# Ordering the second layer's first front, and the first transfers, inside the first layer's plan

## The chip, the core and the metric
The kernel runs on one core of one Trainium2 chip. The metric is the device time of one execution in microseconds, as the median of the runs. The engines named below are TensorE (PE, with its weight loads as PEld), VectorE (DVE), ScalarE (ACT), GpSimd (POOL) and SyncE (SP), which issues most of the DMAs; ACT issues the others. Each engine runs its instructions in the order in which the program gives them.

## What is computed
All data are float32: x is 32 batches of 128 tokens of 512. Layer 0 is a cross attention with 32 query heads and 8 key heads of width 16, layer 1 an RWKV block with a state per head of 16 x 16.
```python
# layer 0, per batch
q = x @ Wq + bq;  k = ctx @ Wk + bk;  v = ctx @ Wv + bv
attn = softmax(q k^T / sqrt(16) + mask)
x = layernorm((attn v) @ Wo + bo + x) * gamma + beta
# layer 1, time mixing
xn = ln1(x);  sx = shift(xn) - xn
xxx = xn + sx * maa_x
m = tanh(xxx @ maa_w1) by 5;  x_i = xn + sx * (maa_stack_i + m_i @ maa_w2_i)   # w, k, v, r, g
w = exp(-exp(time_decay + tanh(x_w @ decay_w1) @ decay_w2))
# per token: out = r (state + u k v);  state = w * state + k v
x = x + groupnorm(out) * silu(g) @ Wo
# layer 1, channel mixing
x = x + sigmoid(xr @ ffn_Wr) * (relu(xk @ ffn_Wk)^2 @ ffn_Wv)
```

## The kernel before
**Tiling.** The 32 batches go in 16 groups of two (NG, G), so most tiles are 128 partitions by 4 chunks by 256 tokens. Layer 0 (`attend`, L483) runs over all groups and leaves its rows in DRAM (`x1d`); layer 1 (`load1`, `front`, `recurrence`, `tail`, L977 to L1436) runs over all groups after it and loads these rows again.

**The planner.** Nothing is issued where it is written. `Plan.add` (L176) records a step: its engine, a cost in us, a function that issues its instructions, and the tiles that it reads and writes. `give_out` (L238) then simulates the five engines and issues the steps in the order which it finds; that order is kept on the chip, as it stands within `manual_schedule`. For each engine it takes, among the steps whose inputs are done and whose tiles have room, the one that can start without waiting 0.3 us or more, and among these the one with the lowest due. A due is the group's number plus an offset from a table written out by hand (WHEN0 at L34 for layer 0, WHEN1 at L68 for layer 1). A step of any engine but SP may be taken only if its due is no more than `ahead` (15.2739 in layer 0, 13.2672 in layer 1) over that of the oldest step still open. Layer 1's plan also lowers the dues of steps that others wait for, and gives places in the order of the dues (`turns`, L224); layer 0's plan does not.

**Two plans.** Layer 0's plan (`pl`) holds the attention alone and is given out whole; layer 1's plan is made after it, in tile pools taken after those of layer 0 are released. On each engine every step of the second plan therefore comes behind every step of the first.

**Around the junction.** The last steps of a group in layer 0 are: rd and bc (softmax sums to DRAM and back, SP L701, L707), oT (POOL L711), pw (PE L716), x (DVE L719), the norm (`norm`, L385: statistics on DVE, root on POOL), z (POOL L407, L721, L722) and the store of x1d (SP L724). A group of layer 1 begins with the load of its rows (x1t, SP L974) and state (s0), then `front` (L998): both norms, `shift` (L843: transposes pxnt, xnt on ACT, sxt on POOL), `mixed` (L888: xx on ACT and POOL), ph (PE L924), h (ACT L1009), the inputs x for i = 1 and 0 (`x5s`, L1010: px on PE L1025, DVE L1041, an add on POOL L1055), pdd (PE L1090) and hd (ACT L1095). The heavy projections follow: pk, pv, pr, pg (`project2`, PE L938), the inputs 2, 3 and 4, and the storing of v (vd, SP L1105), which the recurrence fetches again (kv, SP L1230).

**The start.** Outside the plan, SP loads ident, col, wk, wv, bk, ev, bv, the three rows, and prev; ACT loads wq and wo, and then the weights of layer 1 (w1, w2, wd1, wd2, wk1, wr1, wo1, wv1, wg1, fv). The loads of the plan (x, ct and m of each group) come behind those of SP. These instructions outside the plan are placed by the compiler between the plan's steps. wv1 and wg1 are loaded into `wtmp` (3 places, two chunks each) and copied by POOL (L759).

Of the kernel before, what the change touches and what calls it, by code (L numbers as in the profile page):

```python
# [8 lines left out]
F32 = mybir.dt.float32  # L9
# [5 lines left out]
P = 128  # L15
B = 32
# [19 lines left out]
        oT 0: -2.6252, oT 1: 3.3357, pT 0 0 0: -0.1744, pT 0 1 0: 1.2267, pT 1 0 0: -1.9192, pT 1 1 0: -0.8740,  # L36
        pr 0 0 0 0: 0.6529, pr 0 0 0 1: -0.0746, pr 0 0 1 0: -4.0682, pr 0 0 1 1: -0.1561, pr 0 1 0 0: 0.4501,
        pr 0 1 0 1: -0.3203, pr 0 1 1 0: -0.7878, pr 0 1 1 1: 0.0820, pr 1 0 0 0: 1.7871, pr 1 0 0 1: 2.2002,
        pr 1 0 1 0: -0.8730, pr 1 0 1 1: -1.8966, pr 1 1 0 0: -0.4270, pr 1 1 0 1: -2.0592, pr 1 1 1 0: 3.7724,
        pr 1 1 1 1: -0.8531, qT 0: -0.5042, qT 1: -0.0255, qT 2: -0.2635, qT 3: -1.0961, xT 0: 0.4768, xT 1: -0.1677  # L40
    """,
    "DVE": """
        kT 0: 1.2690, kT 1: -3.2473, mx 0 0 0: -1.1417, mx 0 0 1: -0.2864, mx 0 1 0: 1.2620, mx 0 1 1: -2.6166,
        mx 1 0 0: 2.6711, mx 1 0 1: -0.5335, mx 1 1 0: 1.7226, mx 1 1 1: -0.3724, pT 0 0 1: -1.2967, pT 0 0 2: 0.0513,
        pT 0 0 3: 0.0848, pT 0 1 1: -8.6724, pT 0 1 2: 0.0095, pT 0 1 3: -0.9150, pT 1 0 1: 0.2278, pT 1 0 2: 1.5335,
        pT 1 0 3: 0.1265, pT 1 1 1: -0.6521, pT 1 1 2: 0.0264, pT 1 1 3: -1.1512, pprev: -0.5247, pr 0 0 0: 3.0552,
        pr 0 0 1: -0.2034, pr 0 1 0: -6.8992, pr 0 1 1: 0.0841, pr 1 0 0: 3.8180, pr 1 0 1: 5.4106, pr 1 1 0: -0.1859,
        pr 1 1 1: -1.0387, pv: 1.4494, rT 0: 1.7614, rT 1: -6.4827, rs 0: 0.0025, rs 1: -1.3038, st a 0: 3.4819,
        st a 1: -0.7930, x 0: -1.6215, x 1: -0.7745
    """,  # L50
    "PE": """
        pk: -1.2090, po 0 0: -0.9547, po 0 1: -1.2559, po 1 0: 1.2553, po 1 1: -6.5573, ppT 0 0 0: -3.2574,
        ppT 0 0 1: -3.1897, ppT 0 0 2: 0.0759, ppT 0 0 3: -0.0050, ppT 0 1 0: -5.1850, ppT 0 1 1: -1.0390,
        ppT 0 1 2: -1.3378, ppT 0 1 3: -0.1908, ppT 1 0 0: -0.7659, ppT 1 0 1: 0.2863, ppT 1 0 2: -2.6538,
        ppT 1 0 3: -0.7327, ppT 1 1 0: -1.0396, ppT 1 1 1: -1.1030, ppT 1 1 2: -1.7141, ppT 1 1 3: -1.3304,
        pprev: 0.5587, pq 0: -0.5900, pq 2: -0.5203, pv: -0.7591, pw 0: -0.0622, pw 1: 0.0036, pxT 0: -1.1551,
        pxT 1: -1.2087, sc 0 0: -0.4025, sc 0 1: -0.1903, sc 1 0: 0.0128, sc 1 1: 0.3141
    """,
    "POOL": """
        oT 0: 1.2881, oT 1: 3.1556, sd a 0: -1.3405, sd a 1: -6.4837, x 0: -1.9469, x 1: 2.5134, z 0: -5.8626,  # L60
        z 1: -2.1882
    """,
    "SP": """
        bc 0: -0.4187, bc 1: -0.5237, ct 0: -1.3394, ct 1: -1.7142, m 0: -0.3457, m 1: 0.1999, rd 0: -8.2177,
        rd 1: 2.2127, x 0: -1.7606, x 1: -2.6917, z 0: 0.8576, z 1: -0.5330
# [4 lines left out]
        att 0: 8.9413, att 1: 10.3245, att 2: 10.9514, att 3: 4.2202, ew 0: 3.0530, ew 1: 7.1294, ew 2: 5.4799,  # L70
        ew 3: -0.1804, gt 0: 2.7896, gt 2: 7.2564, h0: 4.2793, hd: -0.7228, kk 0: 1.5652, kk 2: 8.9401,
        kv 0 0 0: 2.8237, kv 0 0 1: 2.8350, kv 0 1 0: 6.5988, kv 0 1 1: 4.7931, kv 1 0 0: 11.5248, kv 1 0 1: 12.1370,
        kv 1 1 0: 8.1713, kv 1 1 1: 8.4770, kv 2 0 0: 11.3074, kv 2 0 1: 0.7816, kv 2 1 0: 10.6862, kv 2 1 1: 7.1872,
        kv 3 0 0: 19.3264, kv 3 0 1: 5.1004, kv 3 1 0: 5.3317, kv 3 1 1: 6.5296, pk 0: 7.8527, pk 2: 3.7734,
        pv 0: 2.8655, pv 2: 13.4147, r 0: 10.0348, r 2: -0.1824, rr 0: 13.0999, rr 1: 2.8864, rstd: 5.6019,
        sq 0: -0.0986, sq 1: 8.8327, sq 2: 0.5974, sq 3: 5.6588, w4 0: 6.7771, w4 1: 3.1835, w4 2: 6.2518,
        w4 3: 1.3276, xnc 0: 5.1909, xnc 1: 3.5402, xnc 2: 5.5512, xnc 3: 9.4093, xnt 0: 4.3436, xnt 1: 6.3722,
        xnt 2: 7.1367, xnt 3: 8.6670, xx 0: 11.9355, xx 1: 6.5413, xx 2: 5.6875, xx 3: 9.8818, yk 0: 11.1356,
        yk 1: 1.7804, yk 2: 15.8112, yk 3: 13.9956, yr 0: 7.4657, yr 1: 8.8095, yr 2: 3.2938, yr 3: 8.7878,
        zc 0: 7.6581, zc 1: 0.9023, zt 0: 10.9657, zt 1: 5.2637  # L80
    """,
    "DVE": """
        a 0 0: -0.5883, a 0 1: -0.2414, a 0 2: 0.1043, a 0 3: 8.0118, a 1 0: 7.0047, a 1 1: 12.1762, a 1 2: 5.6912,
        a 1 3: 9.0685, a 2 0: 9.3322, a 2 1: 6.5083, a 2 2: 6.9110, a 2 3: 0.9712, a 3 0: 7.3177, a 3 1: 7.6874,
        a 3 2: 2.3097, a 3 3: 12.5406, ar 0 0: 2.4656, ar 0 1: 9.7666, ar 0 2: 5.7906, ar 0 3: 7.9178, ar 1 0: 6.6300,
        ar 1 1: 1.2202, ar 1 2: 6.5895, ar 1 3: 8.7855, ar 2 0: 28.3612, ar 2 1: 16.5392, ar 2 2: 12.3754,
        ar 2 3: 11.7973, ar 3 0: 9.1129, ar 3 1: 12.3189, ar 3 2: 9.0665, ar 3 3: 1.8400, gn 0: 8.4672, gn 1: 5.8193,
        gn 2: 3.6790, gn 3: 6.5194, gt 0: 0.0430, gt 2: -0.3529, own 0: 7.8602, own 1: 10.0300, own 2: 6.6987,
        own 3: 5.2960, pb 0: 0.7953, pb 1: 8.4093, pb 2: 4.1923, pb 3: 8.8563, raw 0: 2.2489, raw 1: 0.4033,
        raw 2: 5.9725, raw 3: 6.8204, rk 0: -0.4021, rk 1: 1.1444, rr 0: 7.1091, rr 1: 5.2378, rstd: 2.3485,  # L90
        st c 0: 6.9368, st c 1: 1.2521, st t 0: 8.7646, st t 1: 7.8543, x1c 0: 1.0294, x1c 1: 6.6954, x5 0 0: 2.9930,
        x5 0 1: 7.2539, x5 0 2: -1.0976, x5 0 3: 11.6924, x5 1 0: 8.4707, x5 1 1: -0.2943, x5 1 2: 10.2532,
        x5 1 3: 6.3221, x5 2 0: -0.6575, x5 2 1: 6.4713, x5 2 2: 12.8297, x5 2 3: 15.9903, x5 3 0: 6.5967,
        x5 3 1: 6.3600, x5 3 2: -0.8402, x5 3 3: -0.6696, x5 4 0: 8.4589, x5 4 1: 12.8956, x5 4 2: -0.4045,
        x5 4 3: 5.3981
    """,
    "PE": """
        acc 0: 13.3710, acc 1: 6.5427, acc 2: 6.5657, acc 3: 5.8187, pb 0: 18.0159, pb 2: 13.4697, pc 0: 0.6934,
        pc 1: 3.6234, pc 2: 5.2455, pc 3: 6.5762, pd 0: 1.0255, pd 1: 5.0703, pd 2: 6.9998, pd 3: 6.9286, pdd: 8.4674,
        pew 0: 6.2963, pew 2: 8.3876, pg 0: 1.2658, pg 2: 11.7555, ph0: 5.5651, pk 0: -0.5984, pk 2: -0.5853,  # L100
        pkk 0: 6.0318, pkk 2: 6.3700, pkv 0: 3.8400, pkv 1: 1.5996, pr 0: 0.4302, pr 2: -0.2452, prr 0: 3.2418,
        prr 1: 6.5661, pv 0: 20.6763, pv 2: -0.4713, pvar: 9.0706, pwo 0: 6.3422, pwo 1: 7.2520, px5 1 0: 6.5332,
# [226 lines left out]
def xattn_rwkv_kernel(  # L329
# [91 lines left out]
    with ExitStack() as sa:  # L421
# [8 lines left out]
        for tag in ("ln_st", "ln_mv", "ln_sd"):  # L430
            pl.tag(tag, 2)
# [1093 lines left out]
```

## Time and profile before
| | before |
|---|---|
| median of 3 runs | 2157.05 us (2153.24 to 2163.01) |
| the profiled execution | 2150.95 us, span 2149.2 us |
| busy: PE, PEld | 1992.6 us (93%), 1305.8 us (61%) |
| busy: DVE, ACT, POOL | 1783.0 us (83%), 1058.0 us (49%), 1294.0 us (60%) |
| mean granted clock of PE | 0.962 |
| DMA, mean rate | 252.23 MB, 117 GB/s |

The span runs from the first to the last instruction; some 2 us lie outside it. In the page's slices each digit is the busy share of one fortieth of the span (54 us) in tenths, and PEclk is the clock that the throttle granted to PE. A row of busy time by stretches gives, after the bounds and the length, for each engine the busy us and the number of instructions, then the granted clock, the mean busy share of the 16 DMA engines, and GB/s. A row of the timeline gives start, us, engine, line and operation, out<-in, and in brackets the idle time before it with what ended it; merged rows have one start and one length. "SPq" and "ACTq" are those engines' issuing of DMAs.

### The profile page before, as it was taken

The page shows a single profiled execution, that of the slowest core. Times are in us where ns is not written, and L with a number is a line of the kernel's source. Part 1 is how long each engine was busy: PE and PEld are TensorE (multiplying, and loading weights), DVE is VectorE, ACT ScalarE, POOL GpSimd, SP SyncE. Part 2 cuts the span into 40 slices and gives each one's busy share as a digit, 9 for nine tenths or more (in the row PEclk, how much of TensorE's full clock was granted, in tenths as well). Part 3 has the DMA queues.
Part 4 walks back from the last instruction along what each step waited for, and adds up shares of the span by engine and source line. Part 5 has one row for each costly group of instructions (what it writes and reads, how often), then busy time and mean ns, then how long its engine had stood idle before and what let it go on. Part 6 is the DMA issues. An engine that isn't in the chain of part 4 may idle for free.

```text
span 2149.2 us, 36169 instructions
## 1 busy us (share of the span) xinstructions
PE 1992.6 (93%) x11908; PEld 1305.8 (61%) x11908; DVE 1783.0 (83%) x2182; ACT 1058.0 (49%) x3473; POOL 1294.0 (60%) x1081
## 2 busy tenths in 40 slices
PE   5999999999958779999999999999999999999977
PEld 4666666666626546566675665656657566575643
DVE  3888888888844888989988899898988989888881
ACT  3888888888842233433434434344343443433332
POOL 1273334343345666777777777777777877777552
PEclk9999999999978889999999999999999999999988
DMA  7232221221024687887977978879788797886851
GB/s 207 61 127 66 62 70 60 68 61 60 27 81 80 114 121 114 146 158 122 175 122 138 167 117 168 130 138 163 120 161 134 141 165 117 162 136 115 163 99 59
DMA packets 155883, 252.23 MB, mean 117 GB/s; under 512 B 50512, under 2 KB 97648, under 8 KB 139312
## 3 DMA queue, kind: packets, MB, share of 16 engines
q1 hardware_dynamic: 149232, 240.27, 59.8%
q10 hardware_dynamic: 6464, 9.66, 1.4%
q8 instruction: 94, 1.54, 0.4%
q14 instruction: 93, 0.76, 0.1%
HBM read 224.12 MB, written 25.69 MB: 116 GB/s over the span
## 4 chain that ended last, share of the span: by engine, by line
PE 52%; DVE 7%; ACT 2%; DMA 1%; issue 1%; POOL 0%; SPq 0%; POOLq 0%; DVEq 0%; ACTq 0%
PE pkk L938 5%; PE pwo L956 5%; PE pk L938 5%; PE pv L938 5%; PE pr L938 4%; PE acc L1296 4%; PE pkv L956 4%; PE pg L938 4%; PE prr L956 4%; DVE a L1267 3%; PE pdd L1090 2%; PE px L1025 2%; DVE x L1041 2%; PE pc L1321 1%; PE pew L1162 1%
## 5 line engine op out<-in xcount | busy, mean ns | idle before, releaser
L1252 POOL TENSOR_TENSOR kv<-kv,kx 128x1016 f32<-128x1016 f32 x256 | 597.6, 2349 | 142.9 <-DMA kv<-vd 63.1
L1267 DVE TENSOR_TENSOR_SCAN a<-w,kv 128x1024 f32<-128x1024 f32 x256 | 587.3, 2294 | 29.1 <-ACT w L1191 8.0
L653 ACT ACTIVATE pr<-pr,mx 128x128 f32<-128x128 f32 x1024 | 398.3, 391 | 53.4 <-DVE mx L641 47.0
L1281 DVE TENSOR_TENSOR ar<-a,r 128x1024 f32<-128x1024 f32 x256 | 311.5, 1217 | 4.4
L1055 POOL TENSOR_TENSOR x<-x,xnt 128x512 f32<-128x512 f32 x160 | 187.2, 1181 | 92.1 <-DVE x L1041 79.4
L653 ACT ACTIVATION_READ_ACCUMULATOR pr<-pr,mx 128x1 f32 x1024 | 193.7, 189 | 0.0
L1041 DVE SCALAR_TENSOR_TENSOR x<-px,col,sxt 128x256 f32<-128x256 f32 x320 | 133.9, 473 | 59.5 <-PE pdd L1090 37.2
L629 DVE TENSOR_TENSOR pr<-sc,m 128x1024 f32<-128x1024 f32 x128 | 153.7, 1210 | 32.1 <-PE sc L613 29.0
L665 PE MATMUL ppT<-ident,pr 128*128 128x128 f32 x1024 | 154.3, 281 | 12.1 <-DVE pT L672 4.3
L665 PEld LDWEIGHTS ppT<-ident,pr 128*128 128x128 f32 x1024 | 115.4, 141 | 77.9 <-issue 25.9
L641 DVE TENSOR_REDUCE mx<-pr 128x8 f32<-128x1024 f32 x128 | 155.5, 1215 | 2.7
L1296 PE MATMUL acc<-ar,give 128*32 128x256 f32 x2048 | 142.5, 394 | 12.6 <-DVE ar L1281 12.6
L672 DVE COPY pT<-ppT 128x512 f32<-128x512 f32 x192 | 128.3, 682 | 22.9 <-PE ppT L665 18.2
L397 POOL TENSOR_SCALAR sd_a<-mv_a 128x1 f32<-128x1 f32 x32 | 7.1, 223 | 214.6 <-DVE mv_a L393 214.5
L716 PE MATMUL pw<-wo,oT 128*128 128x512 f32 x256 | 122.3, 610 | 9.8 <-POOL oT L711 8.8
L938 PE MATMUL pkk<-yk,fk 128*128 128x256 f32 x512 | 121.4, 392 | 6.2 <-POOL yk L905 6.2
L956 PE MATMUL pwo<-wo,gt 128*128 128x512 f32 x256 | 122.2, 612 | 5.0 <-ACT xnt L868 2.9
L938 PE MATMUL pr<-x,wr 128*128 128x256 f32 x512 | 122.0, 387 | 3.8 <-DVE x L1041 3.8
L557 PE MATMUL pq<-xT,wq 128*128 128x256 f32 x512 | 122.9, 389 | 0.7 <-ACT xT L512 0.7
L938 PE MATMUL pk<-x,wk 128*128 128x256 f32 x512 | 123.3, 390 | 0.0
L956 PE MATMUL pkv<-fv,kk 128*128 128x512 f32 x256 | 120.3, 603 | 0.0
L938 PE MATMUL pg<-x,wg 128*128 128x256 f32 x512 | 117.6, 383 | 2.9 <-DVE x L1041 2.9
(146 smaller groups left out, 3714.7 us busy)
## 6 DMA issues: line engine op xcount, KB each, us to landing
kv<-vd SPq DMA_DIRECT2D x1024, 128.0 KB
fk<-in_fWkT_dram SPq DMA_DIRECT2D x16, 1024.0 KB
fr<-in_fWrT_dram SPq DMA_DIRECT2D x16, 1024.0 KB
x<-in_x_dram SPq DMA_DIRECT2D x32, 256.0 KB
ct<-in_ctxT_dram SPq DMA_DIRECT2D x32, 256.0 KB
bc<-rd SPq DMA_DIRECT2D x256, 32.0 KB
x1d<-z SPq DMA_DIRECT2D x32, 256.0 KB
x1t<-x1d SPq DMA_DIRECT2D x32, 256.0 KB
```

Of the source, the lines that this page charges most:

```text
L629: lambda b=b, sc=sc, jp=jp, pr=pr: nc.vector.tensor_tensor(pr(), sc()[:, 2 * jp : 2 * jp + 2].rearrange("p j g e s -> p (j g e) s"), ms[b] ...
L641: lambda pr=pr, mx=mx: nc.vector.tensor_reduce(mx(), pr(), AX.X, ALU.max, negate=True),
L653: nc.scalar.activation(pr()[:, 4 * i + h, :], pr()[:, 4 * i + h, :], AF.Exp, bias=mx()[:, 4 * i + h : 4 * i + h + 1], accum_out=sm()[:, h0 ...
L665: nc.tensor.transpose(pt()[:, h, :], pr()[:, 4 * i + h, :], ident)
L938: nc.tensor.matmul(pp()[:, i], (w() if isinstance(w, Cell) else w)[:, kc, (c + i) * P : (c + i + 1) * P], flat(src()[:, kc]), start=(kc == 0),
L956: nc.tensor.matmul(pp(), src()[:, c, b, :], (w() if isinstance(w, Cell) else w)[:, c, :], start=(c == 0), stop=(c == KC - 1),)
L1041: lambda i=i, c=c, pp=pp, half=half: nc.vector.scalar_tensor_tensor(flat(ts[i]()[:, c]), pp()[:, half], col[:, MS0 + i, c : c + 1], flat(s ...
L1055: lambda i=i, c2=c2: nc.gpsimd.tensor_add(ts[i]()[:, c2 : c2 + 2].rearrange("p c b t -> p (c b) t"), ts[i]()[:, c2 : c2 + 2].rearrange("p ...
L1252: lambda c=c, kv=kv, e=e: nc.gpsimd.tensor_tensor(kv()[:, e, :, :, 1:T], kv()[:, e, :, :, 1:T], k()[:, c, :, 0 : T - 1].unsqueeze(1).broad ...
L1267: lambda kv=kv, a=a, e=e: nc.vector.tensor_tensor_scan(a().rearrange("p j b t -> p (j b t)"), w4().rearrange("p j b t -> p (j b t)"), kv() ...
L1281: lambda c=c, a=a, ar=ar: nc.vector.tensor_tensor(ar(), a().rearrange("p j b t -> p j (b t)"), flat(r()[:, c]).unsqueeze(1).broadcast_to([ ...
L1296: nc.tensor.matmul(acc()[32 * j : 32 * j + 32, :N], give[:, d].rearrange("p e h -> p (e h)"), tiles[d]()[:, j], start=(d == 0), stop=(d == 3),
```

## The change
Layer 1's plan object (`pl1`) and the pools of the tiles which the front needs are made before layer 0's, and layer 0's plan takes these pools in too: tags g, z, ln_st, ln_mv and ln_sd become shared, ct takes places of sx, and prev one of z. `front` becomes a generator that stops before the k projection. For group 0 its first part, with that group's loads, is added to layer 0's plan after all groups of the attention; the second part, inputs 2, 3 and 4 included, is added to layer 1's plan. The loads of wk, wv, wo, bk, ev, bv, rows and prev become steps of the plan on SP, and so do w1, w2, wd1 and wd2 (one step of six DMAs, moved from ACT's queue). Both tables of offsets and both `ahead` values are new; steps carry a default due, used where a table has no entry. `wtmp` has one place of one chunk.
```diff
@@ the tables (a few of the lines)
 WHEN0 = {
     "ACT": """
...
+        xT 0: -4.1567, xT 1: 1.6257, xnt 0: 17.9453, xnt 1: 13.6560, xnt 2: 9.3695, xnt 3: 16.3747, xx 0: 16.6506,
+        xx 1: 12.5462, xx 2: 9.3077, xx 3: 10.8186, zt 0: -0.6012, zt 1: 17.8612
...
+        pdd: 14.8434, ph0: 13.8237, pk: 1.1577, po 0 0: -4.9799, po 0 1: 2.0137, po 1 0: -2.0040, po 1 1: -4.7406,
...
+        ppT 0 1 1: 0.7530, ppT 0 1 2: -6.4545, ppT 0 1 3: -6.8061, ppT 1 0 0: -2.6161, ppT 1 0 1: -3.6615,
...
+        px5 1 0: 18.8360, px5 1 2: 17.3205, pxT 0: 0.9389, pxT 1: 1.0851, pxnt 0: 14.7081, pxnt 2: 16.4922,
...
+        bc 0: 3.2700, bc 1: -4.0132, bk: -1.2899, bv: 2.7605, ct 0: -0.5080, ct 1: -0.6118, m 0: 0.7228, m 1: 1.1452,
+        prev: 18.4768, rd 0: -1.5286, rd 1: -2.3089, rows: 0.9971, s0 0: 2.5007, s0 1: 17.0661, w1: 18.8761,
+        wk: -3.3755, wo: 11.9829, wv: 2.0257, x 0: -1.5799, x 1: -0.7466, x1t 0: 1.3447, x1t 1: -0.8892, z 0: -6.3176,
...
@@ Plan
-        s.due = s.group + self.when[s.key]
+        s.due = s.group + self.when.get(s.key, due - s.group)
...
     def give_out(self):
+        for _, _, live in self.pools.values():
+            live[:] = [c for c in live if any(u.end is None for _, _, u in c.uses)]
+            for c in live:
+                for _, _, u in c.uses:
+                    u.end = u.end and 3.4
@@ pools
+    pl1 = Plan(ctx, tc, WHEN1, 20.0126)
+    for tag, bufs in (("xt", 2), ("s0", 3), ("z", 3), ("xn", 2), ("sx", 2), ("x5", 4), ("h0", 1), ("hd", 1)):
+        pl1.tag(tag, bufs)
...
-        wt = sa.enter_context(tc.tile_pool(name="wt", bufs=3))
-        pl = Plan(sa, tc, WHEN0, 15.2739)
+        wt = sa.enter_context(tc.tile_pool(name="wt", bufs=1))
+        pl = Plan(sa, tc, WHEN0, 9.8213)
         pl.turns = False
+        pl.pools.update(pl1.pools)
@@ first transfers
-        wk = load_w(Wk, P, "wk", wa, nc.sync)
-        wv = load_w(Wv, P, "wv", wa, nc.sync)
-        wo = load_w(Wo0, E, "wo", wa, nc.scalar)
...
+        def later(name, t, move, go, due):
+
+            c = Cell(None, None, name, t=t)
+            pl.add("SP", 0.5, go, w=[c], of=f"{name}_0", due=due, move=move)
+            return c
+
+        def weight(w, width, name, due):
+            t = wa.tile([P, KC, width], F32, name=name)
+            return t, later(name, t, width / 85, lambda: nc.sync.dma_start(t, w.rearrange("(c p) m -> p c m", p=P)), due)
+
+        wk, wk_c = weight(Wk, P, "wk", -0.9)
+        wv, wv_c = weight(Wv, P, "wv", -0.7)
+        wo, wo_c = weight(Wo0, E, "wo", -0.2)
...
+        prev_c = pl.cell("z", [T, E], "prev_0")
+        pl.add("SP", 0.5, lambda: nc.sync.dma_start(prev_c()[: 2 * B], prev), w=[prev_c], due=0.5, move=0.7)
...
-            ct = pl.cell("ct", [P, KC, G, T], f"ct_{gr}")
+            ct = pl.cell("sx", [P, KC, G, T], f"ct_{gr}")
@@ front
-    def front(g):
+    def front(g, D):
...
+        yield
         g.k, g.v = kx[gr % 2], vx[gr % 2]
-        heads(xk, wk1, g.k, 0, "k")
-        xv, xr = x5s((2, 3))
+        heads(xk, wk1, g.k, 0, "k", D + 0.4)
+        xv, xr = x5s((2, 3), D + 0.5)
@@ after the attention
         for gr in range(NG):
             attend(gr)
+
+
+        def first_weights():
+            for t, w in ((w1, maa_w1), (wd1, decay_w1)):
+                nc.sync.dma_start(t, w.rearrange("(c p) m -> p c m", p=P))
+            nc.sync.dma_start(w2, maa_w2[0:P, :])
+            nc.sync.dma_start(wd2[0:64], decay_w2)
+            for at in (64, 96):
+                nc.sync.dma_start(wd2[at : at + 32], maa_w2[P:160, :])
...
+        w1_c = later("w1", w1, 5.0, first_weights, 2.0)
+        add, cell = pl.add, pl.cell
+        first = load1(0, NG - 2.0)
+        first.w = [w1_c]
+        ahead = front(first, NG - 1.5)
+        next(ahead)
         with tc.manual_schedule():
             pl.give_out()
...
-            for half in range(2):
-                tmp = wt.tile([P, 2, E], F32, tag="wtmp", name=f"wtmp_{n}{half}")
+            for c in range(KC):
+                tmp = wt.tile([P, E], F32, tag="wtmp", name=f"wtmp_{n}{c}")
@@ at the end
-    pl = Plan(ctx, tc, WHEN1, 13.2672)
+    pl = pl1
...
-    groups = [load1(gr) for gr in range(NG)]
-    front(groups[0])
+    groups = [first] + [load1(gr, gr - 2.0) for gr in range(1, NG)]
+    for _ in ahead:
+        pass
     for gr in range(NG):
         if gr + 1 < NG:
-            front(groups[gr + 1])
+            for _ in front(groups[gr + 1], gr):
+                pass
         recurrence(groups[gr])
         tail(groups[gr])
```

## The prediction
> **What bounds the kernel now.** I read the page's slices first, then busy time by stretches, then the timeline at the two places where TensorE (PE) is idle. One profiled execution took 2150.95 us, span 2149.2. The first two lines below are the page's slices; the others are stretches (bounds and length, then busy us of PE, PEld, DVE, ACT, POOL, the granted clock, DMA share, GB/s).
> ```profile
> PE   5999999999958779999999999999999999999977
> ...
> PEclk9999999999978889999999999999999999999988
> ...
> 0.00:20.00 20.00, 2.31 (x10) 1.62 (x11) 1.28 (x9) 1.87 (x2) 1.80 (x8) 1.00 0.91 273
> 20.00:40.00 20.00, 19.09 (x112) 15.96 (x113) 6.61 (x12) 5.01 (x18) 4.43 (x4) 1.00 0.86 248
> 400.00:500.00 100.00, 99.60 (x761) 69.31 (x760) 90.08 (x131) 86.29 (x392) 39.39 (x47) 1.00 0.23 68
> 600.00:613.00 13.00, 12.01 (x64) 5.32 (x63) 9.06 (x13) 9.35 (x47) 2.03 (x2) 1.00 0.13 42
> 613.00:620.00 7.00, 0.20 (x5) 0.17 (x2) 0.82 (x3) 0.59 (x1) 5.49 (x7) 0.67 0.22 69
> 620.00:627.00 7.00, 6.36 (x8) 2.35 (x8) 0.60 (x1) 0.00 (x0) 0.00 (x0) 0.60 0.02 8
> 627.00:640.00 13.00, 0.45 (x1) 0.18 (x1) 3.83 (x12) 1.04 (x2) 8.03 (x14) 0.58 0.47 115
> 640.00:662.00 22.00, 16.13 (x81) 9.91 (x81) 5.90 (x15) 5.22 (x12) 10.78 (x10) 0.63 0.23 73
> 969.00:1058.00 89.00, 86.55 (x475) 56.19 (x474) 79.73 (x90) 35.50 (x79) 66.13 (x51) 0.98 0.83 144
> ```
> PE is the bound: 99.6 of 100 us in layer 1, 86.55 of 89 in a second-layer group. It is idle 17.7 us at the start, and between 613 and 662 it works little, at a clock near 0.6. The timeline shows why (start, us, instruction):
> ```profile
> 11.76 1.05 SPq L490 DMA_DIRECT2D x<-in_x_dram  x2
> ...
> 18.23 1.08 PE L506 MATMUL pxT<-ident,x 128*128 128x128 f32 x4 [0.83 <-DMA x<-in_x_dram]
> ...
> 618.59 15.04 SPq L724 DMA_DIRECT2D x1d<-z  x2
> 619.83 0.50 PEld L716 LDWEIGHTS pw<-wo,oT 128*128 128x128 f32 x2 [7.28 <-POOL oT L711]
> 619.83 6.53 PE L716 MATMUL pw<-wo,oT 128*128 128x512 f32 x8 [6.80 <-POOL oT L711]
> ...
> 633.74 0.86 SPq L974 DMA_DIRECT2D x1t<-x1d  x2
> ...
> 636.50 0.69 DVE L392 BATCH_NORM_STATS2 st_t<-x1t 128x6 f32<-128x512 f32 x1 [7.37 <-DMA x1t<-x1d]
> ...
> 661.76 3.72 PE L938 MATMUL pk<-x,wk 128*128 128x256 f32 x16
> ```
> At the start the first x is issued only at 11.76, as the twelfth transfer on SP. At the junction SP stands 15.04 us with the last group's x1d store, and the load of group 0's x1t, whose data were written hundreds of us earlier, stands behind it. Then group 0's front runs alone: 636.50 to 661.76 with no heavy matmul.
>
> **The junction, part by part.** Moved into the first plan: group 0's x1t and s0 loads, both norms, pxnt, xx, ph, h, px and x for inputs 0 and 1, pdd, hd. PE durations come from one undisturbed second-layer group (1000 to 1089): pxnt 2.41/2 = 1.21, ph 1.89, px 16 of 40 x 5.86 = 2.34, pdd 3.45; sum 8.9 us. On the others, from the rows in 636 to 661: DVE 2 norms + 8 x at 0.43 = 5.5, ACT 6.3, POOL 2 roots + sxt 2.0 + xx 2.3 + x 4 x 1.18 = 11.
>
> What disappears: from the end of the last pw (626.36) to pk (661.76) lie 35.4 us. Not all comes back:
> - px for inputs 2 and 3 stays in the second plan (2.3 us of PE), though before it ran inside that stretch. Its POOL adds (2 x 1.18 for xv) and the zeroing of vx (1.85) now queue behind the last z on POOL, which ends at 633.25; so xv stands at about 636 and v is copied at about 640.5 where it was 669.6. The recurrence, which needs v stored by SP and fetched again, moves by 29 us. SP is free from 633.7, before that store.
> - The clock. The Trainium skill (TensorE: Matmul & The Clock Gate, Part 1) lets the full clock return after some 3.4 us of sustained work. Here pw ran its eight matmuls at half pace through all of 6.53 us, and px/pdd, working from 650.17, reached full pace only near 659.4, 9.2 us on. By the rule pk starts warm; by the rows its first 2.7 us are slow, 1.35 us lost. I take the rows; it is inside the 29.
>
> What the 8.9 us cost where they go. They can lie beside nothing in steady layer 1 (PE 99.6%), so the upper price is 8.9. The lower is below nothing: PE is idle 1.0 + 6.8 + 0.6 us between 600 and 627, and work there would keep the clock up, so that pw takes 3.4 instead of 6.5 us: -3. Where they go is read from the code: a step may run only within 9.82 dues of the oldest open one. zt 1 (17.86) opens when the oldest is 8.04, in group 14's second half; px5 (18.84) at 9.02, after group 15's first transposes (15 - 6.81 = 8.19). So most fall in the last group, and with later dues than nearly all its PE steps they win PE only when those would wait over 0.3 us; ph (13.82) and pdd (14.84) compete evenly, 5.3 us. I take 2. DVE (90%) and ACT (86%) have room for 5.5 and 6.3 us over two groups of 35 us; POOL's 11 us are covered while it is 39% busy, and if they stood ahead of the last oT they would cost up to 4.7 (four x adds).
> Junction: 29 - 2 = 27 saved, ends 29 - 8.9 - 4.7 = 15 and 32.
>
> **The start.** SP's order by due becomes wk, x 0, bk and ev, x 0', ct, next x, ct; rows (3.77 us of issue), bv, prev and wo come later, m too. ACT's queue keeps wq, and wk1 now stands second where wo stood. Ahead of x's end are 64 + 34 + 256 + 256 KB on SP, and about as much of wq by the other queue: 1.2 MB at the 370 GB/s seen in the early 1.5 us slices is 3.3 us after 2 us in which little moved (0 and 139 GB/s), so pxT near 6 instead of 18.2; pq needs all of wq, 1 MB beside as much of SP's, near 8 or 9 instead of 21.46. That is 12 us at best. Against it: ACT's third transfer waited from 1.76 to 10.97[...], and ACT's first copy of pxT stands in the same order behind such issues (in the trace ACT was through with them at 17.7). If wr1 and some of wo1 are put ahead of the copy, it waits to 11 to 18. And m, moved behind x, ct and rows, must be there for the first pr (34.93 before). I take 8, ends 0 and 13.
>
> **The rest.** wtmp has one buffer instead of three, and eight loads instead of four; each but the first waits on ACT for POOL's copy (1.07 us) of the one before. That engine is 82% busy between 60 and 200, PE waited 3.2 us there for it; queued behind would be exps and then the transposes. Nearest row: POOL's 2.51 us wait for wtmp_g. Seven such waits are 17 us if nothing covers them, 0 if each issue comes after the copy; I take 2, nearer to the trace's spacing of 3.4 to 5.8 us between these issues. The w1 to wd2 loads leave ACT for SP: six issues of about 0.5, on a queue with room, 0. prev, ct, z in shared places: no added instruction, 0. All other dues and both look-aheads are new. Layer 1 can gain at most its 0.4% (2 us); in layer 2 there are 2.2 us idle in each group, some 30 between 680 and 800 and 30 after 2000, which a different order may shrink or widen: plus or minus 10, taken as 1 lost.
>
> **Sum.** 27 + 8 - 2 - 1 = 32 saved: 2150.95 becomes 2119. The profiled run lay 6.1 under the median of the runs shown; against that median: 2157.05 - 32 = 2125.
>
> **Rivals.**
> 1. Both gains come, likeliest (0.53): 2125, its own range 2108 to 2140.
> 2. The front pays full price and the start gives nothing (0.21): 15 to 20 at the junction, less 2 lost: about 2141. For it: layer 1's PE is full, ACT's issues stand before the copy. Against: look-ahead and dues put the front in the drain.
> 3. More than this (0.06): junction 32, start 13, layer 2's idle falls by 10: 55 less 2 lost, 2157 - 53 = 2104.
> 4. Nothing measurable (0.10): the wtmp waits stand uncovered (17) and layer 2 gives back 10: 32 - 15 more - 9 = 8 saved, 2149.
> 5. Slower (0.10). One mechanism: the new second-layer order on DVE. In steady groups PE has one wait, pdd for DVE's x, 27.6 us over 13 times (2.1 each). If a scan and its multiply (2.29 + 1.22 = 3.5 us) come before those x, the wait grows by as much in each of 15 groups: 52 lost, 2125 + 52 = 2177. It turns the sign at 2.1 us a group and counts as slower (over 2168) from 2.9. For it: the wider look-ahead, 13.27 to 20.01, and DVE 90% busy. Against: the order in which one group feeds the next is not changed by the code, only by dues.
>
> "Faster" means under 2146, "slower" over 2168; about 0.5% is what a measurement can tell. Case 1 and 3 are faster, two thirds of case 2, a third of 4: 0.53 + 0.06 + 0.14 + 0.03 = 0.76; slower 0.10 and 0.01 of 4; the rest 0.13. The range 2102 to 2152 leaves out case 5, part of 4 and half of 3.
>
> **What would show it.** Right: first pxT near 6 to 8 and pq by 10 to 14; px and pdd between 570 and 620 (less the start's shift); no idle PE beyond 10 us between the last pw and pk; pk within 3 us of that pw; the same 88.7 us per group. Wrong: ACT's first copy behind queue issues after 15; pw's wait for oT longer than 6.8 with POOL busy on x; ACT's wtmp issues followed by idle PE; a PE wait over 5 us in each second-layer group.

## The result, and the profile after
The changed kernel takes 2161.15 us (median of 20 runs, 2154.78 to 2170.48); the kernel before, on the same chip, 2154.91 (20 runs, 2147.78 to 2165.08). The ratio is 1.0029, 95% interval 1.0015 to 1.0042: no faster, 6 us slower, where 32 saved were forecast. The profiled execution took 2161.51 us, span 2159.7, mean granted clock 0.956 (0.962 before).

The page's slices of the changed kernel, PE and its clock:
```profile
PE   6989999999987779999999999999999999999987
...
PEclk9989999999988769999999999999999999999988
```
The first slice is fuller than before and the hollow at the junction is still there. But the third slice has a loss that before did not have: an 8 at a clock of 8. The stretches show it in numbers (columns as in the prediction):
```profile
0.00:20.00 20.00, 8.61 (x28) 6.90 (x29) 0.57 (x5) 2.99 (x5) 1.37 (x8) 1.00 0.96 314
20.00:40.00 20.00, 16.71 (x104) 13.31 (x103) 11.88 (x14) 9.63 (x43) 4.82 (x4) 0.97 0.78 190
100.00:200.00 100.00, 87.17 (x612) 56.00 (x608) 75.89 (x119) 68.49 (x315) 53.12 (x56) 0.93 0.30 93
400.00:500.00 100.00, 98.81 (x772) 67.24 (x771) 89.05 (x127) 84.49 (x385) 40.09 (x48) 1.00 0.21 64
1000.00:1089.00 89.00, 86.57 (x480) 56.17 (x476) 79.31 (x89) 34.96 (x77) 66.09 (x51) 0.98 0.80 143
```
The steady stretches of both layers stand as before. From 100 to 200 us PE is busy for 87.17 us with 612 instructions; in the kernel before the same stretch has 95.62 us and 737:
```profile
100.00:200.00 100.00, 95.62 (x737) 65.34 (x736) 84.78 (x133) 82.46 (x374) 56.32 (x58) 1.00 0.31 98
```
In this trace the last matmul of the last pw begins at 644.8 instead of 625.8. The last pw's of groups 1, 3 and 13 (counted from 0) already come 14, 21 and 22 us late: nearly all of the loss is made in the first four groups, up to 222 us.

The timeline of the changed kernel, at the start and from the last pw to the first fetch of the recurrence (start, us, instruction):
```profile
2.10 0.80 SPq L888 DMA_DIRECT2D x<-in_x_dram  x1
...
10.72 1.94 PE L905 MATMUL pxT<-ident,x 128*128 128x128 f32 x8 [10.72 <-DMA x<-in_x_dram]
...
640.55 4.80 PE L1125 MATMUL pw<-wo,oT 128*128 128x512 f32 x8
...
649.18 5.41 PE L544 MATMUL pk<-x,wk 128*128 128x256 f32 x16
...
661.27 0.57 ACT L683 COPY vx<-pv 128x512 f32<-128x512 f32 x1
...
661.91 12.62 SPq L719 DMA_DIRECT2D vd<-vx  x16
...
674.57 1.39 SPq L1314 DMA_DIRECT2D kv<-vd  x3
```
Both places that the forecast aimed at did improve. x is issued at 2.10 instead of 11.76, and pk follows the last pw after 3.8 us instead of 35.4. What was gained is lost elsewhere: in the first layer, between vx and the first scan, and behind it. Between vx and the first scan SP stores v with sixteen DMAs before it fetches any of it, which takes 12.62 us. For 2.5 us of these, from 667.09 to 669.55, SP stands until the second copy of vx is done. Before the change it issued eight and then fetched:
```profile
669.62 5.15 SPq L1105 DMA_DIRECT2D vd<-vx  x8
```

A table of a few landmarks (us, last matmul of the last pw; first copy of vx; first scan of the recurrence; end of the span) divides the difference:

| kernel | last pw | vx | first scan | end |
|---|---|---|---|---|
| before | 625.8 | 669.0 | 688.1 | 2149.2 |
| changed | 644.8 | 661.3 | 688.9 | 2159.7 |
| stage by stage, changed less before | +19.0 | -26.7 | +8.5 | +9.7 |

Where part of the +19.0 is lost shows on ACT and POOL (timeline of the changed kernel):
```profile
114.16 5.90 POOL L1184 TENSOR_SCALAR wo<-wo 128x512 f32<-128x512 f32 x4
...
120.00 1.03 POOL L1177 COPY wv<-wtmp_v 128x512 f32<-128x512 f32 x1
...
121.07 0.37 ACTq L1176 DMA_DIRECT2D wtmp_v<-in_WvT_dram  x1
...
121.47 0.58 ACT L1077 COPY pT<-ppT 128x512 f32<-128x512 f32 x1 [7.55 <-POOL sd_t L410]
...
122.11 1.51 PE L1084 MATMUL po<-pT,v 128*32 128x256 f32 x12 [4.87 <-ACT pT L1077]
```
ACT stands 7.55 us. The profile names sd_t, which is merely POOL's next instruction. Ahead of the copy of pT in ACT's order stands the DMA into wtmp_v at 121.07. It needs the one staging place free, so it needs the end of POOL's copy (121.03), and that copy stood behind POOL's 5.90 us scaling of wo. The copy of pT queues behind the DMA on ACT, and PE waits 4.87 us for pT. The Trainium skill (DMA: Bandwidth & Descriptors, Anatomy of one DMA) says, in a section on DMAs that GpSimd issues, that the DMA engines do not wait on semaphores: such a wait is made by the sequencer that issues, ahead of dispatch. This trace agrees, on ACT: it is idle for 7.55 us, and the issue comes 0.04 us after POOL's copy ends.

### The profile page after: what moved, and what is told of

It reads as the page before. It is cut to its first block, busy times and chain, and to the rows that moved or that the text cites. A ratio compares the mean times of both kernels' runs of the same rounds, so it can differ in the third digit from the quotient of the medians.

```text
span 2159.7 us, 36243 instructions
## 1 busy us (share of the span) xinstructions
PE 2008.4 (93%) x11908; PEld 1307.7 (61%) x11908; DVE 1787.3 (83%) x2182; ACT 1051.1 (49%) x3473; POOL 1293.8 (60%) x1081
## 4 chain that ended last, share of the span: by engine, by line
PE 66%; DMA 11%; DVE 10%; POOL 4%; ACT 3%; issue 3%; SPq 2%; POOLq 0%; ACTq 0%; DVEq 0%
DMA kv<-vd 6%; PE pw L1125 5%; PE pk L544 5%; PE pkk L544 5%; PE pwo L562 5%; PE pv L544 5%; PE pq L960 4%; PE ppT L1072 4%; PE pg L544 4%; PE acc L1384 4%; PE pr L544 4%; DVE a L1353 3%; PE pkv L562 3%; PE prr L562 3%; PE sc L1018 3%
## 5 line engine op out<-in xcount | busy, mean ns | idle before, releaser
L544 PE MATMUL pv<-x,wv 128*128 128x256 f32 x512 | 117.7, 383 | 2.4 <-POOL x L666 2.4
L562 PE MATMUL prr<-fr,yr 128*128 128x512 f32 x256 | 117.6, 593 | 1.8 <-DMA fr<-in_fWrT_dram 1.8
```

Of the source, the lines that this page charges most:

```text
L544: nc.tensor.matmul(pp()[:, i], (w() if isinstance(w, Cell) else w)[:, kc, (c + i) * P : (c + i + 1) * P], flat(src()[:, kc]), start=(kc == 0),
L562: nc.tensor.matmul(pp(), src()[:, c, b, :], (w() if isinstance(w, Cell) else w)[:, c, :], start=(c == 0), stop=(c == KC - 1),)
```

## The experiments
Two theories from the traces. A: the saving at the junction is real, and is lost in the first layer where ACT and POOL stand at the issues and copies of the second layer's weights, which lie outside the plan. B, the rival: the moved steps (the front) pay full price in the first layer, whose new order is slower by itself, and the second layer's new order takes the rest. All ratios are to the kernel before on the same chip, with 95% intervals; landmarks are from one profiled execution each.

| run | median us | ratio | last pw | first scan | end |
|---|---|---|---|---|---|
| a_host | 2153.50 | 0.9994 (0.9984 to 1.0003) | 635.5 | 679.6 | 2149.4 |
| b_host | 2151.89 | 0.9982 (0.9975 to 0.9990) | 623.1 | 685.2 | 2149.2 |
| b_wt1 | 2159.08 | 1.0019 (1.0011 to 1.0027) | 631.6 | 694.1 | 2154.5 |
| a_when1 | 2157.48 | 1.0009 (0.9999 to 1.0019) | 645.3 | 689.5 | 2153.2 |
| e5_old_order | 2150.14 | 0.9960 (0.9948 to 0.9973) | 634.5 | 678.6 | 2144.6 |
| e6_vd_after | 2146.51 | 0.9947 (0.9935 to 0.9960) | 635.9 | 680.0 | 2144.3 |
| e7_both | 2148.24 | 0.9956 (0.9943 to 0.9968) | 635.1 | 679.2 | 2150.7 |
| e8_front_behind | 2177.01 | 1.0085 (1.0071 to 1.0099) | 629.7 | 709.3 | 2181.4 |
| e9_weights_spread | 2138.85 | 0.9923 (0.9906 to 0.9941) | 630.4 | 674.6 | 2137.5 |
| e10_before_spread | 2150.25 | 0.9973 (0.9965 to 0.9980) | 622.3 | 686.5 | 2148.3 |
| e11_start_alone | 2154.56 | 0.9997 (0.9987 to 1.0008) | 624.6 | 687.3 | 2148.4 |
| e12_copies_first | 2144.63 | 0.9950 (0.9935 to 0.9964) | 636.4 | 680.9 | 2140.0 |
| e13_fine | 2136.66 | 0.9906 (0.9889 to 0.9923) | 620.1 | 664.2 | 2130.5 |
| e14_fine_copies | 2128.52 | 0.9868 (0.9849 to 0.9887) | 621.8 | 660.7 | 2127.0 |
| e15_fine_front_behind | 2164.15 | 1.0041 (1.0025 to 1.0057) | 620.5 | 697.7 | 2161.0 |
| e16_change_loads_moved | 2138.79 | 0.9911 (0.9896 to 0.9927) | 621.0 | 665.1 | 2131.5 |
| e17_change_best | 2128.64 | 0.9862 (0.9846 to 0.9878) | 619.2 | 658.2 | 2130.9 |
| e18_best_old_order | 2133.82 | 0.9875 (0.9853 to 0.9896) | 622.5 | 661.5 | 2138.8 |

**The staging tile: a_host, b_host, b_wt1.** In the first two, wv1 and wg1 come from the host in the order in which they are needed, so that the reordering on the chip is left out (so too in all runs from e5 to e15 and in e18); b_wt1 is the kernel before with the change's one place of one chunk.
```diff
-        for src, dst, n in ((WvT, wv1, "v"), (WgT, wg1, "g")):
-            for c in range(KC):
-                tmp = wt.tile([P, E], F32, tag="wtmp", name=f"wtmp_{n}{c}")
...
+        wv1 = load_w(WvT, E, "wv1", cp, nc.scalar)
+        wg1 = load_w(WgT, E, "wg1", cp, nc.scalar)
```


> After, with wv1 and wg1 laid out by the host and loaded straight into their places: no wtmp, no copies on POOL, two issues on ACT instead of eight. Theory S (staging): the one-place wtmp holds ACT until POOL has copied, and PE loses what lies idle between 100 and 200 (12.8 us against 4.4 before); then this kernel is 8 to 12 us under after, 2149 to 2153, and PE is idle 3 to 5 us in that stretch. Theory F (front): what the after kernel loses in layer 1 comes from the front's 8.9 us of PE and the new dues; then the idle time moves elsewhere and the time is within 3 us of after.

> The control for it: before, with the same host layout of wv1 and wg1. Before had three places of two chunks and no long wait there. Theory S expects 0 to 3 us under before (fewer issues on ACT). Theory F the same. If it gains as much as the after kernel does, the gain is that of fewer instructions and not of the wait.

> Before, with only the staging tile of after: one place of one chunk, eight loads. Theory S expects 6 to 12 us over before, with an ACT wait of 3 us or more behind a wtmp load. Theory F expects 0 to 3 us over before.

The change loses 9.3 us at the last pw to its staging (644.8 to 635.5), before only 2.7 (625.8 to 623.1); given the change's tile, before loses 8.5 (631.6 against 623.1). So the tile as it stood, with its loads and copies, is one cause, and costs either kernel about the same. Theory S named the cause, and its sizes only in part: b_wt1 lies, by its ratio, 4.1 us over before where 6 to 12 were expected, and a_host's PE is still idle for 9.1 us between 100 and 200 where 3 to 5 were. The tile is not the whole: without it the last pw still comes 12.4 us later than b_host's. Part of that shows in a_host's trace as another such stand: ACT is idle for 4.37 us ahead of a copy of pT at 128.07, the issue of a constant row (127.72) stands just before that copy, and PE waits 4.62 us for it. What that issue waited for is not shown.

**The second layer's order: a_when1, e5_old_order** (the second with a_host's layout).
```diff
-    pl1 = Plan(ctx, tc, WHEN1, 20.0126)
+    pl1 = Plan(ctx, tc, WHEN1, 13.2672)
```
with the table WHEN1 of before as well.

> After, with the second layer's table and look-ahead of before. Theory O (the new second-layer order costs time: the kernel falls back by 6 us between the first and the last group of layer 2, and kv is fetched only after all four vd are stored) expects 5 to 12 us under after. Against it: the old order does not help, since the second layer is bound by PE in every group; then within 3 us of after.

> Beside the kernel with wv1 and wg1 laid out ahead of the launch (2153.5 us), only the second layer's table of offsets and its look-ahead are those of before. Theory: the new order of the second layer costs about 4 us by itself (it did with the staging tile in place: 2161.2 to 2157.5), so 2149.5. Rival: with the staging tile gone the loss is no longer there, because it was the same lost time seen twice: 2153 to 2154.

Medians fall by 3.7 us (2161.15 to 2157.48) and 3.4 (2153.50 to 2150.14); by the ratios, each to its own chip's kernel before, by 4 and 7. By these two the new order costs some 4 to 7 us; e7 and e18 will not bear it out.

**The store of v ahead of its fetch: e6_vd_after, e7_both** (e7 with before's order as well).
```diff
+    one = {s.key: s for s in pl.steps if s.group == 0}
+    for key in ("SP vd 2", "SP vd 3"):
+        one[key].before.add(one["SP kv 0 0 0"])
+        one["SP kv 0 0 0"].behind.append(one[key])
```


> Beside the kernel with wv1 and wg1 laid out ahead of the launch (2153.5 us), only group 0's storing of v on SP is changed: the last two quarters of it (8 of the 16 DMAs) follow the first fetch of v instead of standing ahead of it. Theory: the first fetch starts 6 to 7 us earlier and the whole second layer with it: 2146.5 to 2147.5. Rival: the ramp of the second layer is bound by the fetches' own transfers, and what the first of them gains is given back by the eighth step of the recurrence: 2153 to 2154.

> The two edits together, old order of the second layer and the first fetch ahead of half of the storing of v. Theory: the gains add, 4 and 7 of 2153.5, so 2142.5. Rival: only the order counts, 2149 to 2150; the first recurrence step early, the 32nd at the place of the run without the fetch's edit.

The size of e6 was as expected, the way was not: the first fetch is issued at 658.4 instead of 665.3, yet the first scan stays (680.0, 679.6). The gain comes later, between the first and the sixteenth scan (73.7 us instead of 79.3). In e7 the gains do not add: 2148.24, near the rival's value. What holds the first scan in e6 is ACT:
```profile
675.53 1.50 ACT L499 ACTIVATE xx<-sxt,col 128x256 f32<-128x256 f32 x3
676.94 0.29 ACT L1318 COPY kv<-s 128x8 f32<-128x8 f32 x2
...
680.02 2.30 DVE L1344 TENSOR_TENSOR_SCAN a<-w,kv 128x1024 f32<-128x1024 f32 x1 [4.43 <-POOL kv L1328]
```
The copy of the state into the fetched tile shows no idle time before it: it comes directly behind the next group's xx.

**The front's own price: e8_front_behind.** In give_out the group's steps keep their places in the simulation, but are issued after the last of the attention.
```diff
+            held.append((s, new))
+            if s not in hold:
+                self.issue(*held.pop())
...
+        for s, new in held:
+            self.issue(s, new)
```


> Beside the kernel with both edits, the first group's steps up to its mixed inputs are issued behind the last group's attention (the loads of its rows and state stay where they are), and the order of the attention itself is the same. Theory: in their places they had cost the first layer their full price, 9 us of PE and 2 to 4 of waiting, and had saved some 29 us behind the last pw; so the last pw comes 11 to 13 us earlier than in the kernel with both edits, the pk 35 us after it instead of 4 to 6, and the end 16 to 19 us later. Rival 1: they cost the first layer more than that (a slower clock, places held), up to the full 19 us seen at the last pw; then the end is 8 to 12 us later. Rival 2: nothing of it reaches the end: within 2 us of the kernel with both edits.

Neither sum was right. The last pw comes 5.4 us earlier, but 42.4 us lie between it and pk, and the end comes 28.8 us later. So moving the front ahead is worth what was forecast, and theory B's first half falls. But without the front this first layer still ends 6.6 us later than b_host's: something else in it is slow.

**Where the weights are issued: e9_weights_spread, e10_before_spread.** On top of e6 (and of b_host), the second layer's weights and constant rows go from ACT to SP, one load per group from the third group on, and the work on them to later groups.
```diff
+        def beside(s):
+            if s.key == "PE pw 1" and s.group in todo:
+                for go in todo.pop(s.group):
+                    go()
```


> Beside the run with the first fetch ahead of half of the storing of v (2146.5 us), the second layer's weights and constant rows are no longer issued by ACT from 20 us on, but by SP, one after each group of the attention from the third on, and POOL's and DVE's work on them comes behind the ninth to thirteenth group; the order of everything else is the same. Theory: what the first layer lost between 100 and 200 us (PE busy 91 of 100 us, against 98 in the kernel before with the same layout ahead of the launch) was ACT standing at these issues and the transfers of POOL's scalings; so PE is busy 97 or more there, the last pw comes at 626 to 629 instead of 636, and the end at 2137 to 2140. Rival: the attention's new order loses it by itself; the last pw within 2 us of 636 and the end at 2145 to 2148.

> The same spreading of the second layer's weights put into the kernel before (with wv1 and wg1 laid out ahead of the launch, 2151.9 us). Theory: before loses little to these issues (PE busy 98 of the 100 us from 100 on), so at most 3 us: 2149 to 2152, last pw 620 to 623. Rival: it loses as much as the changed kernel, and both gain 7 to 9.

Theory A held for 100 to 200 us (PE busy 97.89) and for the end, and the last pw came at 630.4, just outside 626 to 629; before gained next to nothing at its last pw (622.3, b_host 623.1). But e9's last pw's of groups 5, 6, 10 and 11 slipped again. There the timeline has up to sixteen of these DMAs on SP between rd and bc, the two transfers by which the softmax sums are spread: at one of them rd ends at 453.84 and bc begins at 459.62. In e10 such blocks cost nothing, but there they stand ahead of rd (one from 408.59 to 414.4, rd at 416.13), not between rd and bc. So the pair shows that the place matters; whether the new order also has less slack ahead of bc is not shown.

**The start alone: e11_start_alone.** In b_host, x and ct go ahead of wv, bv, rows and wo.
```diff
+            if count[0] == 12:
+                nc.sync.dma_start(wv, Wv.rearrange("(c p) m -> p c m", p=P))
+                nc.sync.dma_start(bv_bc, bv.broadcast_to([P, P]))
```


> One part of the change alone: in the kernel before (with wv1 and wg1 laid out ahead of the launch, 2151.9 us), the first rows of x and ct are issued ahead of wv, bv, the three rows and wo, as in the changed kernel; all else is as before. Theory: the first pq starts 7 to 8 us earlier, and all of it reaches the last pw (615 to 616 instead of 623) and the end: 2144 to 2145. Rival: the transfers put back are missed at their new places, or the time is lost again where the second layer's weights come in, as in the changed kernel: last pw 620 to 623 and the end 2149 to 2152.

The stretch from 20 to 40 us, then the row of PE's waits in the first 60 us (us, times, longest):
```profile
20.00:40.00 20.00, 13.78 (x76) 11.58 (x75) 4.81 (x10) 2.58 (x8) 3.33 (x3) 0.83 0.79 251
```
```profile
PE pv L595 <- DMA wv<-in_Wv_dram: 5.7, 1, 5.7
```
The rival's reason held: 8.32 us of work in the first 20 us instead of 2.40, and 13.78 instead of 19.09 in the next. PE, started earlier, waits for wv, which was put back. The outcome was a little worse than the rival's: last pw 624.6, and by the ratios 3 us behind b_host. The order of the attention is the old one here, which asks for pv at once; so this shows only that the start's gain does not pass by itself.

**The first scan: e12_copies_first.**
```diff
+    for late, soon in (("ACT xnt 0", "ACT kv 0 0 1"), ("POOL sxt 0", "POOL kv 0 0 1")):
+        two[late].before.add(one[soon])
```


> Beside the run with the first fetch ahead of half of the storing of v (2146.5 us), in the second layer's first group the copies of the state into the first two fetched tiles (ACT) and their products (POOL) are put ahead of the next group's xnt and sxt. Theory: there the first scan stood at 680 behind the next group's steps on ACT, 8 us after its data had come; now it starts at 671 to 673, and the end comes 5 to 8 us earlier, 2139 to 2141. Rival: the ramp is bound by the fetches; the first scan comes early, the eighth at 714 to 716 as in that run, and the end at 2145 to 2148.

The edit held back one of the four xnt; the others went ahead, and the first scan stood at 680.9. So it does not answer its question, and against e6 the ratio shows no difference.

**Loads behind bc: e13_fine, e14_fine_copies, e15_fine_front_behind.** e13 is e9 with each load behind a bc in small blocks; e14 adds e12's edit for all four xnt and both sxt, e15 adds e8's.
```diff
+            behind(2 + i, "SP bc 1", load, t, w)
+        for d in range(S):
+            behind(2 + d // 4, "SP bc 0", load_wo1, d)
+            behind(7 + d // 4, f"SP bc {d // 2 % 2}", load_rows, d)
```


> Beside the run with the second layer's weights spread over SP (2138.9 us): there the blocks of up to 16 of these DMAs stood on SP between the storing of the softmax sums (rd) and their spreading (bc), and the last pw's of groups 5, 6, 10 and 11 slipped by 10 to 12 us in all. Here each stands behind a bc, in blocks of four to six at most, and POOL's scalings one by one behind its oT. Theory: the new order has no slack ahead of bc, and behind it the loads cost nothing; the last pw comes at 620 to 624 instead of 630, the end at 2129 to 2133. Rival: it is the transfers that hold the new order up, wherever they are issued; last pw 628 to 631, end 2137 to 2140.

> The kernel with the loads behind each bc, and in the second layer's first group the first two copies of the state (ACT) and their products (POOL) ahead of all four of the next group's xnt and both sxt (in the run with the copies ahead of the next group's first steps, only the first of the four was put back, and the first scan did not move). Theory: the first scan starts 6 to 8 us earlier after the first vx than without it (27.6 us there, 19 in the kernel before), and 4 to 6 of it reach the end: 2125 to 2128. Rival: the fetches bind the ramp, and the next group's steps that are put back are late later: end within 2 us of the kernel without it.

> The kernel with the loads behind each bc, with the first group's steps up to its mixed inputs issued behind the last attention group. It shows what these steps cost the first layer where nothing else disturbs it. Theory: 5 to 9 us, as in the pair with and without them before (5.4 us at the last pw), so the last pw at 613 to 617 and the end 26 to 30 us later than without the edit. The forecast's own value was 2: last pw 618 to 622, the end 32 or more later.

e13's last pw is at 620.1, where theory put it (its median is 4 us above the expected, its profiled execution within). So it was how the loads stood on SP, not their transfers. e15 then gives the front's price in an undisturbed layer: last pw 620.5 without it, where theory expected 613 to 617, and 620.1 with it, in one execution each. In this pair it is free: without it the last pw stands 5.84 us waiting for oT, with it PE has the front's pdd to do there, and no wait for oT shows. It is worth 27.5 us at the end (2164.15 to 2136.66). In e14 the scan follows the copies at once:
```profile
660.37 0.31 ACT L1337 COPY kv<-s 128x8 f32<-128x8 f32 x2
660.70 2.30 DVE L1363 TENSOR_TENSOR_SCAN a<-w,kv 128x1024 f32<-128x1024 f32 x1
```
22.4 us after the first vx (638.3) instead of 27.6, and the ratio falls from 0.9906 to 0.9868.

**One edit to the change itself: e16_change_loads_moved, e17_change_best, e18_best_old_order.** e16 keeps the changed kernel's staging tile, layout, second-layer order and store of v; only the second layer's loads and the work on them move. The loads go from ACT to SP, behind bc; POOL's copies and scalings go behind oT, DVE's copies behind x. e17 adds the edits of e6 and e14. e18 is e14 with before's second-layer order.
```diff
-                nc.scalar.dma_start(tmp, src[c * P : (c + 1) * P])
-                nc.gpsimd.tensor_copy(
...
+            behind(5 + i, "SP bc 1", stage, src, i % KC, f"wtmp_{n}{i % KC}")
+            behind(6 + i, "POOL oT 0", unstage, dst, i % KC)
```


> The changed kernel itself (2161.2 us) with one edit: the second layer's weights and constant rows are no longer issued by ACT from 1 us on, but by SP behind each bc of the attention from the third group on, and POOL's copies out of the one staging tile and its scalings stand behind its oT, one at a time; the staging tile, the order of the second layer and of the storing of v are as in the change. Theory: neither the staging tile nor the moved steps cost the first layer anything by themselves; its loss is where the weights' issues and copies stood. So the last pw comes at 620 to 622 instead of 645, and the end 20 to 24 us earlier: 2137 to 2141. Rival: a staging tile of one place costs its 8 to 10 us wherever it is filled: last pw 628 to 631, end 2146 to 2149.

> The same, and in the second layer's first group the first fetch ahead of half of the storing of v, and the copies of the state and their products ahead of the next group's xnt and sxt. Theory: as with the weights laid out ahead of the launch (2128.5 us), since the staging tile costs nothing there: 2127 to 2131. Rival: 8 to 10 us more.

> The fastest kernel so far (2128.5 us: loads behind each bc, copies of the state first, weights laid out ahead of the launch) with the second layer's table of offsets and look-ahead of before. Theory: the new table costs 3.5 to 4 us by itself: 2124 to 2126. Rival: it does so only where the first group comes late (with the first fetch ahead of half of the storing of v the gain was not there: 2148.2 beside 2146.5): 2127 to 2130.

The single edit turns 1.0029 into 0.9911. POOL's groups show part of it; the columns after the bar are busy us, mean ns of one, and idle time just before with what ended it. First the changed kernel, then e16:
```profile
L1177 POOL COPY wv<-wtmp_v 128x512 f32<-128x512 f32 x4 | 4.2, 1055 | 9.0 <-DMA wtmp_v<-in_WvT_dram 9.0
L1177 POOL COPY wg<-wtmp_g 128x512 f32<-128x512 f32 x4 | 4.2, 1054 | 5.1 <-DMA wtmp_g<-in_WgT_dram 5.1
```
```profile
L1228 POOL COPY wv<-wtmp_v 128x512 f32<-128x512 f32 x4 | 4.4, 1091 | 0.0
L1228 POOL COPY wg<-wtmp_g 128x512 f32<-128x512 f32 x4 | 4.3, 1081 | 0.0
```
The same eight copies through the same one place wait 14.1 us in the one and nothing in the other, since each load has some half a group of time before its copy. The stretch from 100 to 200 us in e16, while those loads begin:
```profile
100.00:200.00 100.00, 97.89 (x752) 67.14 (x750) 87.98 (x131) 84.86 (x390) 34.97 (x43) 1.00 0.33 94
```
e17, the change with its loads in place and its first scan freed, beats both kernels: ratio 0.9862, 28.6 us under the kernel before on the same chip (2157.22 to 2128.64). e18's ratio lies within e14's interval: here the second layer's old order brings nothing (its median, 2133.82, lies above both values that were expected).

## Why the prediction was wrong
In the profiled executions 10.5 us were lost, where 32 saved were forecast: 42.5 us apart. Stage by stage: 23.0 up to the last pw (4 saved were forecast there, as 8 - 2 - 2; 19.0 were lost), 2.3 from there to vx (29 and 26.7), 8.5 from vx to the first scan (nothing was forecast), 8.7 behind it (1 lost and 9.7). The first of these decided the outcome, and the step that failed lies in it, with the loads into wtmp and what ACT issues beside them.
- **wtmp: the step that failed.** Taken 2 us, ends 0 and 17. With e16's one edit the changed kernel's last pw comes 23.8 us earlier (644.8 to 621.0), and its end 22.4 (medians 2161.15 and 2138.79; by the ratios 1.2%, 25 us). The bound was made of seven waits for the tile, and its nearest row, one wait of 2.51 us in before, was taken at before's spacing. But these instructions are placed by the compiler, anew for each plan: in the changed kernel POOL's 5.90 us scaling stood ahead of a copy. The sign named for being wrong, an issue into wtmp on ACT followed by idle PE, is the pair of rows at 121.07 and 122.11. The tile took 9.3 us of the 23.8 (a_host). The other 14.5 go when the remaining loads and POOL's scalings move too, and these the bound left out. e16 moves them together, off ACT and to later groups, so their shares are not separated. Rival 4 named uncovered waits, with 17 us; it was given 0.10, and its sum was 2149.
- **The junction: right, with one stretch left out.** From the last pw to vx the changed kernel saves 26.7 us, where 29 were taken. But the step said that with v copied 29 us earlier the recurrence moves by 29; the order behind vx is new too. From vx to the first scan it takes 27.6 us instead of 19.1. Two things queue there, SP's sixteen stores and the next group's steps on ACT. Fetching ahead of half the stores moved nothing at the first scan (e6); with ACT freed as well e17 needs 22.4. No run frees ACT alone, so the stores' own share is open.
- **The front's price: right.** Taken 2, ends 8.9 + 4.7; measured 0.4 below nothing in e13 against e15. In the changed kernel it fell later than foreseen (px from 629.8, pdd 636.98 to 640.6, not 570 to 620), behind a layer that was late. The 5.4 us of e8 came with the disturbance, not with the front alone.
- **The clock: a small term, near in size, its rows misread.** The step set the skill's rule (TensorE: Matmul & The Clock Gate, Part 1) against 9.2 us of slow work from 650.17 on. But in that stretch the clock was at full when px began, and then fell (before, first two rows). The changed kernel does the same (last two rows):
```profile
650.00:652.00 2.00, 1.56 (x10) 1.05 (x10) 0.58 (x2) 0.12 (x1) 0.00 (x0) 1.00 0.00 0
653.00:659.00 6.00, 5.87 (x36) 3.13 (x38) 2.66 (x7) 0.00 (x0) 5.42 (x5) 0.50 0.00 0
```
```profile
643.00:649.00 6.00, 4.72 (x22) 2.42 (x20) 3.42 (x9) 0.00 (x0) 1.55 (x4) 1.00 0.00 0
650.00:653.00 3.00, 3.00 (x8) 2.34 (x8) 2.40 (x8) 0.00 (x0) 3.00 (x4) 0.50 0.02 5
```
So pk did start at full clock, as the rule had it, and lost it on the way: 5.41 us instead of 3.72, 1.7 lost where 1.35 were taken, for another reason. Each fall came after a short wait of px (1.01 us in before, 1.28 in the changed kernel); that the wait made it is not shown. The return took longer than the rule's 3.4 us: the last pw of before worked without a break from 619.83, and the clock stood at 0.50 up to 625.3 (not, as the step had it, to pw's end at 626.36).
- **The start: 8 us came, and hardly any of it was passed on.** pq starts at 13.33, 8.1 us earlier; pxT at 10.72, not near 6. What becomes of it where nothing disturbs the first layer and no front lies in it is seen in e10, with before's start and order, and in e15, with the new ones (PE's work up to 60 us and from there to 600, first e10, then e15):
```profile
0.00:60.00 60.00, 36.48 (x240) 27.94 (x244) 23.01 (x42) 23.37 (x95) 6.20 (x11) 0.97 0.51 146
60.00:600.00 540.00, 531.46 (x4060) 363.69 (x4052) 479.96 (x699) 463.72 (x2117) 213.47 (x246) 1.00 0.24 71
```
```profile
0.00:60.00 60.00, 46.41 (x329) 35.74 (x330) 31.10 (x51) 32.71 (x138) 9.93 (x14) 1.00 0.53 152
60.00:600.00 540.00, 521.21 (x3966) 352.20 (x3966) 475.53 (x693) 456.25 (x2090) 208.24 (x243) 0.99 0.24 72
```
With the new start PE is 9.9 us of work ahead at 60 us, and no longer at 600; the last pw comes 1.8 us earlier (622.3 and 620.5). The lead goes in idle time of the new order. Alone the start gave nothing (e11). The step passed a gain at one wait to the end without asking what PE waits for next. That e16's last pw comes 4.8 us earlier than before's, where 4 were forecast, is luck: 3.5 of it before gains too, when its loads are spread and wv1 and wg1 come laid out (e10).
- **Other dues: taken 1 lost, ends plus and minus 10.** From the first scan to the end the changed kernel takes 1470.8 us, before 1461.1, e16 1466.4. Within the bounds. 4.4 of the 9.7 lie in the first group (87.2 us from its first scan to the next group's, before 82.8), and e6, fetching ahead of half the stores, took 6.6 off a_host's 86.8 there; the cause of the rest stays open. By the ratios two pairs gave the old order 4 and 7 us, two gave it none (e7, e18), and single executions of the later kernels spread over 10 us and more. Rival 5 did not occur: 86.57 us of PE work in the 89 us shown.

The account of e16 against before in their profiled executions closes: 31.5 us saved up to vx (669.0 to 637.5), 8.5 lost up to the first scan, 5.3 lost up to the end, 17.7 in sum (2149.2 to 2131.5). Of the 31.5, 26.7 are the junction's. The change's idea gives that; the place of the second layer's loads, and of the work on them, took it away, and more.

## What to carry to other kernels
When a new order is put on engines that work in order, instructions which lie outside that order (weights loaded for later, their copies and scalings) land anew between its steps: cost each at the worst place, and give it a place of its own, behind a step that nothing waits for. A DMA that waits for its buffer holds all that its issuing engine has queued behind it; load, then copy half a group later, and one buffer is enough. An earlier start or a removed gap is a gain only as far as the next wait, so follow it stage by stage with a few landmarks before summing.

## What the hardware showed unexpectedly
- The issue of a DMA on SP has no one price: in a row, loads of constant rows followed each other by 0.34 us (e9, from 453.89), fetches of v by 0.46, stores of v by 0.63, the last two alike in before and in the changed kernel.
- A block of sixteen loads on SP that put 5.8 us between rd and bc (e9, 453.84 to 459.62) was followed by last pw's that slipped by 3.8 us more and stayed late; a like block ahead of rd (e10, 408.59 to 414.4) was not.
- PE's granted clock fell to 0.83 in a stretch of 20 us (120 to 140 us, changed kernel and a_host) around one wait of 4.6 to 4.9 us for ACT. In the changed kernel it stood at 0.50 from 121 to 127 us, and for 4.89 of these 6 us PE was busy: the wait cost more than its own length.
